# A graph attention layer on one core: x_r and edge attributes in one 64-row product, a last node group of three tiles, all other groups' sums in PSUM, the last group but one from round 772

## The chip, the core and the metric

The kernel runs on one core of one Trainium2 chip. The metric is the device time of one execution in microseconds (us). TensorE (PE) does the matrix products, VectorE (DVE) and ScalarE (ACT) the elementwise work. GpSimd (POOL) issues the indirect DMAs that gather rows by index, and SyncE (SP) issues the other DMAs. PSUM is the memory that PE writes its products to, SBUF the on-chip memory that everything else lies in.

## The reference, cut to what matters

One pre-norm GATv2 layer with a feed-forward part on 12,500 nodes of 128 values and 400,000 edges with 32 attributes each; the edges are sorted by destination. There are 8 heads of 16 channels.

```
h    = relu(layernorm(x)); g = ln1(h)
x_l  = g @ W_l ; x_r = g @ W_r ; e = edge_attr @ W_e
m    = leaky_relu(x_l[src] + x_r[dst] + e, 0.2)      # self loops too, with the mean edge attribute
a    = softmax of (m . att) per head over the edges of a destination
h2   = h + segment_sum(x_l[src] * a) + bias
out  = x + h2 + gelu(ln2(h2) @ W1 + b1) @ W2 + b2
```

## The kernel before, in words

Nodes are padded to 98 tiles of 128. A prologue normalizes all nodes, writes the rows of x_l to DRAM (`xl_dram`) and gathers 116 x 128 raw rows of x. Then `window_edges` works through the edges in 782 pairs. A pair is two units of 256 edges, 512 columns, four gathers of 128 rows. The 29 pairs whose raw rows were gathered in the prologue need no gather: their rows are computed on the way and loaded from `late_dram`.

The order is written out by hand (`tc.manual_schedule`): one Python loop over rounds `r`. In each round every stage works on the pair that `stages` gives it, and each engine takes its instructions in the order in which the loop emits them. For pair c:

- `gather` (round c-4, POOL, L915): four indirect DMAs into `xs`, a ring of 12 buffers. `windows` (round c-3, SP): loads of edge attributes `ea`, of destination differences `dlw` (once for four pairs) and of a window of x_r rows (`xrw`).
- `place` (round c-1, DVE, L945): a one-hot matrix `ne`, bfloat16, of 112 partitions by 512 columns. It compares `dlw` with a column `nid`.
- `combine` (round c, PE): the sum z in PSUM, from four transposes of `xs` (L959), `xrw` x `ne` (L962, bfloat16, x_r held as three bfloat16 parts) and `we_z` x `ea` (L963, float32, two instructions).
- `slope` and `bend` (round c+1): ACT scales z (L969), DVE takes the maximum m (L974).
- `score` (round c+2, PE): `ab` = `farw` x `ne` (L980, which pushes out edges of other units) plus `negrep` x m (L981). `ab` has two PSUM banks in turn.
- `lowest` and `weigh` (round c+3): DVE takes the minimum of `ab` (L988), ACT the exponentials (L999).
- `turn` (c+4, PE, L1007), `keep_turned` (c+5, ACT, L1012), `collect` (c+6, PE, L1021), `own_heads` (c+7, DVE, L1030 and L1036), `put` (c+7, SP, L1047): the weights are turned and multiplied with the rows; each unit's record goes to DRAM (`state`).

Beside this run side jobs, in rounds of their own: `xr_steps` compute x_r for the next four tiles (with a split into three bfloat16 parts, of which `third`, L597, is a DVE subtraction), `raw_steps` do the same for the raw pairs' x_l, and sums over the edge attributes run in the first 196 rounds. When all edges of a group of four node tiles are done, the group's `steps` run over some 20 rounds: `f_load`, scores of the self loops, `f_out` and `f_h` (the softmax sums), statistics, and the feed-forward part up to `f_store` and `f_put`. `f_biases` (L1110, L1112) adds `bias` to `h_sb` and `b2` to `f_x`, and `f_rest` (L1211) adds `h_sb` to `f_x`. There are 25 groups: 24 of four tiles and a last one of two. The last group but one runs a shorter table, `soon`, from round 780 (776 with its loads). The last one runs `last_steps`: loads and self scores in rounds 770 to 775, and the rest, one step after the other, once the last record is in DRAM (round 790).

Of the kernel before, what the change touches and what calls it, by code (L numbers as in the profile page):

```python
# [22 lines left out]
P = 128  # L23
# [17 lines left out]
NS = 3  # L41
# [10 lines left out]
XR_STEPS = 8  # L52
# [49 lines left out]
def node_groups(nt):  # L102

    return [(t, min(GN, nt - t)) for t in range(0, nt, GN)]
# [34 lines left out]
def tile_gnn(  # L139
# [43 lines left out]
    xs_dram = dram.tile([NT * P * NS, P], BF16, name="xs_dram")  # L183
    xs_t = xs_dram.rearrange("(t p s) f -> p t s f", p=P, s=NS)
# [22 lines left out]
    ident_b = const.tile([P, P], BF16, name="ident_b")  # L207
# [12 lines left out]
    we_z = const.tile([P, QP, P], F32, name="we_z")  # L220
    NC3 = NS * CW
# [12 lines left out]
    we_sb = build.tile([P, P], F32, name="we_sb")  # L234
    EP = RU * U
# [10 lines left out]
    def load_consts():  # L246
# [4 lines left out]
        nc.sync.dma_start(we_sb, bass.AP(tensor=w_e.tensor, offset=w_e.offset, ap=[[P, DE], [0, QP], [1, P]]))  # L251
        nc.sync.dma_start(w1_sb, w1)
# [79 lines left out]
    own = build.tile([P, NW, H], F32, name="own")  # L332
    last = build.tile([P, NW, H], F32, name="last")
    third = build.tile([P, CW], F32, name="third")
    in_order = build.tile([P, CW], F32, name="in_order")
    unit = build.tile([P, 1], F32, name="unit")
    fq = build.tile([P, QP, DE], F32, name="fq")
# [3 lines left out]
    def count_up():  # L341
        iota(nc, nh, [[-1, H], [-H, NW]], 0, 1)
        iota(nc, own, [[-1, NW], [0, H]], -NC3, 1)
        iota(nc, last, [[0, NW], [0, H]], -NC3 - NW, 1)
        iota(nc, third, [[-NS, CW]], 0, 1)
        iota(nc, in_order, [[1, CW]])
        iota(nc, unit, [[0, 1]], -NC3, 1)
        iota(nc, fq, [[-1, QP], [-QP, DE]], 0, 1)
        iota(nc, place, [[1, RU]], 0, RU)
        iota(nc, fh, [[-1, H], [-H, C]], 0, 1)  # L350

    def edge_constants():
        nc.vector.tensor_scalar(win_sb, first_sb[:, 0:NU:UP], float(NS * P * 2), None, op0=OP.mult)
        nc.vector.tensor_scalar(first_sb, first_sb, float(H * SH * 4), None, op0=OP.mult)
        nc.vector.tensor_copy(ident_b, ident)
# [14 lines left out]
        nc.vector.tensor_scalar(farw, own, BIG, None, op0=OP.mult)  # L370
        group_range(nc, build, third, NS, CW)
        nc.vector.tensor_mul(third, third, in_order)
        nc.vector.tensor_reduce(nid, third, AX.X, OP.add)
        nc.vector.tensor_scalar(unit, unit, 0.0, None, op0=OP.max)
        nc.vector.tensor_add(nid, nid, unit)
        nc.vector.tensor_scalar(fq, fq, 0.0, None, op0=OP.is_equal)
        qm = build.tile([P, QP], F32, name="qm")
        nc.vector.tensor_reduce(qm, fq, AX.X, OP.max)
        for q in range(QP):
            nc.vector.tensor_scalar(we_z[:, q, :], wer, qm[:, q : q + 1], None, op0=OP.mult)  # L380
# [167 lines left out]
    def xr_steps(pool, bank):  # L548
# [37 lines left out]
        def first(d):  # L586
            n = d["n"]
            xr = d["b"][:, 0 : n * P].rearrange("p (t f) -> p t f", f=P)
            d["parts"] = pool.tile([P, GN, NS, P], BF16, name="xr_parts")[:, 0:n]
            nc.scalar.copy(d["parts"][:, :, 0, :], xr)  # L590
            nc.vector.tensor_sub(tile_of(d, "left", 0), xr, d["parts"][:, :, 0, :])

        def second(d):
            nc.scalar.copy(d["parts"][:, :, 1, :], d["left"][:, 0 : d["n"]])

        def third(d):
            nc.vector.tensor_sub(d["parts"][:, :, 2, :], d["left"][:, 0 : d["n"]], d["parts"][:, :, 1, :])  # L597

        def store(d):
            nc.sync.dma_start(xs_t[:, d["ts"], :, :], d["parts"])  # L600

        return norm, turn, turned, times, first, second, third, store

    def raw_steps(pool, bank):
# [68 lines left out]
        def rows(d):  # L673
            d["xl"] = pool.tile([P, GN, XW], F32, name="l_xl", tag="xr_parts")[:, 0 : d["n"]]
# [90 lines left out]
    with tc.If(fast == 1) as cmp:  # L765
        window_edges(
            tc, n_edges, ea_t, NT, NE, NUE, ident, ident_b, wer, we_z, negrep, diag, nid, farw, bias_r, b2_r, w1_sb, w2_sb,
            cols, xl_dram, xl_t, xs_dram, xs_t, dc_dram, du_dram, late_dram, state, clear, xr_steps, qs, raw_steps, raw, x_t, out_t, h_sb, src_sb, first_sb, win_sb,
        )
    with cmp.Else():  # L770
        any_edges(
            tc, n_edges, dst, dst_tiles, ea_t, NT, NG, NCH, CPP, CP, ident, w_e, att, att_c, bias_r,
            xl_dram, xl_t, xs_t, xr_steps, qs, h_sb, src_sb,
        )
        feed_forward(tc, NT, NG, ident, b2_r, w1_sb, w2_sb, cols, x_t, out_t, h_sb)
# [52 lines left out]
def whole(nc, out, parts):  # L828

    nc.vector.tensor_add(out, parts[:, :, 0, :], parts[:, :, 1, :])  # L830
    for s in range(2, NS):
        nc.vector.tensor_add(out, out, parts[:, :, s, :])


# [9 lines left out]
def window_edges(  # L844
    tc, n_edges, ea_t, NT, NE, NUE, ident, ident_b, wer, we_z, negrep, diag, nid, farw, bias_r, b2_r, w1_sb, w2_sb,
    cols, xl_dram, xl_t, xs_dram, xs_t, dc_dram, du_dram, late_dram, state, clear, xr_steps, qs, raw_steps, raw, x_t, out_t, h_sb, src_sb, first_sb, win_sb,
# [12 lines left out]
    NN = 6  # L859
    NV = WAHEAD + 3  # L860
    NC3 = NS * CW
# [13 lines left out]
    with ExitStack() as es:  # L875
# [13 lines left out]
        xrw = [once.tile([P, P], BF16, name=f"xrw{i}") for i in range(NV)]  # L889
        nes = [once.tile([P, EPR], BF16, name=f"ne{i}") for i in range(NN)]  # L890
        for t in xrw:
            nc.gpsimd.memset(t, 0.0)
        for t in nes:
            nc.vector.memset(t, 1.0)
# [28 lines left out]
        def windows(c):  # L923
            if c % QP == 0:
                ea = load.tile([P, EPR], F32, name="ea")
                nc.sync.dma_start(
                    ea, bass.AP(tensor=ea_t.tensor, offset=ea_t.offset + c * EPR, ap=[[e_pad, DE], [EPR, QP], [1, EPR]])
                )
                n = min(QP * EPR, dc_dram.shape[0] - c * EPR)
                dlw = load.tile([NC3 + NW, QP * EPR], BF16, name="dlw")  # L930
                for rs, dl in ((slice(0, NC3), dc_dram), (slice(NC3, NC3 + NW), du_dram)):
                    nc.sync.dma_start(dlw[rs, :n], dl[c * EPR : c * EPR + n].partition_broadcast(rs.stop - rs.start))
                at = words(win_sb[0:1, c : c + QP], (NT * P - CW) * NS * P * 2)
                for i in range(c, min(c + QP, n_pr)):
                    pairs[i].update(ea=ea, dlw=dlw, win=at[i - c])
            nc.sync.dma_start(
                xrw[c % NV][0:NC3, :].bitcast(U8), rows_at(xs_dram, pairs[c]["win"], NC3, P * 2)
            )

        def place(c):  # L940

            d = pairs[c]
            n, q = sum(edges_of(c)), c % QP * EPR
            ne = nes[c % NN]
            nc.vector.tensor_scalar(  # L945
                ne[0 : NC3 + NW, :n],
                d["dlw"][:, q : q + n],
                nid[0 : NC3 + NW],
                None,
                op0=OP.is_equal,  # L950
            )
            d["ne"] = ne

        def combine(c):
# [7 lines left out]
            nc.tensor.matmul(z[:, :e], xrw[c % NV], d["ne"][:, :e], start=False, stop=False)  # L962
# [860 lines left out]
```

## Time and profile before

| | us |
|---|---|
| three runs | 4013.26, 4021.4, 4024.89; median 4021.4 |
| the profiled execution | 4009.67 |
| its span | 4007.9 |

The page splits the span into busy time by engine, 40 slices, DMA queues, the chain of work that ended last, the costliest groups of instructions and the DMA issues. A row of a group says: line, engine, operation, tiles out and in, count, then busy time, mean of one in ns, and the idle time of the engine ahead of it with what ended it. A row of the timeline says: start, duration, engine, line, operation. The granted clock of TensorE is 0.956 over the span.

| slices of the page | first two | rest |
|---|---|---|
| PE busy, tenths | 3, 4 | 8 or 9, and 7 in the last |
| DVE busy, tenths | 7, 4 | 5 to 7 |
| POOL busy, tenths | 7, 7 | 7, and 3 in the last |

### The profile page before, as it was taken

To read this page: it belongs to the slowest core of one execution; us is meant where nothing else is said; L and a number is where in the kernel's file an instruction comes from. 1 tells how busy PE (TensorE), PEld (TensorE's weight loads), DVE (VectorE), ACT (ScalarE), POOL (GpSimd) and SP (SyncE) were. 2 spreads that over 40 slices of the span, in tenths; PEclk is the share of its full clock that TensorE was granted. 3 is DMA by queue.
4 is the path that set the end of the run, shared out by engine and by line. 5 is a ranking of instruction groups with operands and counts; after the bars stand their busy time and mean duration, and the time that the engine had idled before them with its cause. 6 is when DMAs were issued, how large, how long until landed. Compare 5 with 4: busy or idle time off the path is not lost.

```text
span 4007.9 us, 63213 instructions
## 1 busy us (share of the span) xinstructions
PE 3550.4 (89%) x19116; PEld 2520.3 (63%) x19315; DVE 2540.8 (63%) x5940; ACT 2185.3 (55%) x4768; POOL 2993.8 (75%) x3153
## 2 busy tenths in 40 slices
PE   3488998998889999998998999999989989998997
PEld 3356666666666666666666666666666666666665
DVE  7467676767666665665666666566666656566565
ACT  7445555555555545555555555556555455554554
POOL 7777777777777777777777777777777777777773
PEclk7699999999999999999999999999999999999998
DMA  7677787677656655555556556555556555655553
GB/s 215 207 186 193 197 206 201 173 178 170 166 122 132 128 125 127 126 124 125 118 126 133 125 124 128 128 125 120 127 118 130 125 115 123 127 118 124 125 116 72
DMA packets 650171, 566.02 MB, mean 141 GB/s; under 512 B 385806, under 2 KB 524925, under 8 KB 649581
## 3 DMA queue, kind: packets, MB, share of 16 engines
q1 hardware_dynamic: 549245, 344.42, 34.1%
q0 software_dynamic: 100000, 217.32, 27.4%
q8 instruction: 156, 2.56, 0.3%
q14 instruction: 194, 1.59, 0.1%
q10 hardware_dynamic: 576, 0.13, 0.0%
HBM read 492.44 MB, written 69.02 MB: 140 GB/s over the span
## 4 chain that ended last, share of the span: by engine, by line
PE 43%; DMA 21%; POOL 20%; issue 11%; DVE 1%; ACT 0%; SPq 0%; POOLq 0%; DVEq 0%; ACTq 0%
DMA xs<-xl_dram,src_sb 21%; POOL xs L915 20%; PE z L963 10%; PE acc L1021 9%; PE ab L981 8%; PE pt_ps L1007 5%; PE z L959 5%; PE z L962 2%; PE ab L980 1%; PE acc L1295 1%; PE acc L1270 1%; PE acc L1131 0%; PE pt_ps L581 0%; PE pt_ps L668 0%; PE acc L1126 0%
## 5 line engine op out<-in xcount | busy, mean ns | idle before, releaser
L915 POOL DMA_INDIRECT xs<-xl_dram,src_sb x3009 | 2873.2, 955 | 917.2 <-issue 792.8
L999 ACT ACTIVATE p<-ab,rec 128x256 f32<-128x256 f32 x1563 | 655.2, 471 | 1057.4 <-DVE rec L988 1041.1
L1030 DVE TENSOR_TENSOR own<-acc,diag 128x272 f32<-128x272 f32 x782 | 344.1, 440 | 1077.3 <-PE acc L1021 1061.6
L1021 PE MATMUL acc<-xs,pt 128*128 128x136 f32 x6250 | 881.0, 286 | 2.4 <-DVE f_o L1190 2.2
L959 PE MATMUL z<-ident,xs 128*128 128x128 f32 x3125 | 561.9, 283 | 342.6 <-DMA xs<-xl_dram,src_sb 338.6
L959 PEld LDWEIGHTS z<-ident,xs 128*128 128x128 f32 x3125 | 398.4, 142 | 741.1 <-DMA xs<-xl_dram,src_sb 410.8
L963 PE MATMUL z<-ea,we_z 128*128 128x512 f32 x1564 | 839.7, 620 | 0.1
L981 PE MATMUL ab<-m,negrep 128*128 128x512 f32 x1564 | 802.3, 595 | 11.4 <-issue 1.3
L1021 PEld LDWEIGHTS acc<-xs,pt 128*128 128x128 f32 x6250 | 809.3, 197 | 3.8 <-issue 3.5
L1012 ACT COPY pt<-pt_ps 128x512 f32<-128x512 f32 x782 | 455.1, 582 | 591.0 <-PE pt_ps L1007 581.6
L1007 PEld LDWEIGHTS pt_ps<-ident,p 128*128 128x128 f32 x3125 | 410.9, 147 | 439.3 <-issue 394.4
L988 DVE TENSOR_REDUCE rec<-ab 128x2 f32<-128x512 f32 x781 | 540.4, 692 | 124.0 <-PE ab L981 116.6
L974 DVE TENSOR_TENSOR m<-z,zs 128x512 f32<-128x512 f32 x782 | 532.8, 681 | 87.2 <-ACT zs L969 85.7
L969 ACT ACTIVATE zs<-z 128x512 f32<-128x512 f32 x782 | 472.6, 604 | 44.1 <-DMA xs<-xl_dram,src_sb 35.7
L1007 PE MATMUL pt_ps<-ident,p 128*128 128x128 f32 x3125 | 492.7, 283 | 1.2 <-ACT p L999 1.2
L1036 DVE TENSOR_REDUCE rec<-own 128x34 f32<-128x272 f32 x782 | 340.9, 436 | 26.7
L963 PEld LDWEIGHTS z<-ea,we_z 128*128 128x128 f32 x1564 | 308.1, 197 | 32.7
L981 PEld LDWEIGHTS ab<-m,negrep 128*128 128x128 f32 x1564 | 301.6, 193 | 40.2 <-issue 4.3
L962 PE MATMUL z<-ne,xrw 128*128 128x512 bf16 (+1 forms) x781 | 304.8, 390 | 0.2 <-DMA xs<-xl_dram,src_sb 0.2
L945 DVE TENSOR_SCALAR ne<-dlw,nid 112x512 bf16<-112x512 bf16 x782 | 288.2, 369 | 13.5 <-DMA dlw<-du_dram 13.5
L980 PE MATMUL ab<-ne,farw 128*128 128x512 bf16 x585 | 223.8, 383 | 2.5 <-ACT p L999 1.6
L277 POOL DMA_INDIRECT raw<-in_x,src_raw x116 | 116.6, 1005 | 38.0 <-issue 34.1
(246 smaller groups left out, 2317.4 us busy)
## 6 DMA issues: line engine op xcount, KB each, us to landing
dlw<-dc_dram SPq DMA_DIRECT2D x196, 384.0 KB
ea<-in_ea_t SPq DMA_DIRECT2D x196, 256.0 KB
ea_s<-in_ea_t SPq DMA_DIRECT2D x98, 512.0 KB
xs<-xl_dram,src_sb POOLq DMA_INDIRECT x3009
state<-rec SPq DMA_DIRECT2D x1563, 9.0 KB
xrw<-xs_dram SPq DMA_DIRECT2D x782, 24.0 KB
state<-empty SPq DMA_DIRECT2D x28, 504.0 KB
f_st<-state SPq DMA_DIRECT2D x48, 288.0 KB
```

The lines of the kernel that those rows point to most:

```text
L915: nc.gpsimd.indirect_dma_start(out=xs[:, j, :], out_offset=None, in_=xl_dram, in_offset=bass.IndirectOffsetOnAxis(ap=src_sb[:, c * KP + j ...
L959: nc.tensor.matmul(z[:, j * P : (j + 1) * P], d["xs"][:, j, 0:P], ident, start=(j == 0), stop=False, is_transpose=True)
L962: nc.tensor.matmul(z[:, :e], xrw[c % NV], d["ne"][:, :e], start=False, stop=False)
L963: nc.tensor.matmul(z[:, :e], we_z[:, c % QP, :], d["ea"][:, :e], start=False, stop=True)
L969: nc.scalar.activation(d["zs"][:, :e], d["z"][:, :e], AF.Copy, scale=SLOPE)
L974: nc.vector.tensor_tensor(d["m"][:, :e], d["z"][:, :e], d["zs"][:, :e], op=OP.max)
L981: nc.tensor.matmul(ab[:, :e], negrep.rearrange("p n h -> p (n h)"), d["m"][:, :e], start=False, stop=True)
L988: nc.vector.tensor_reduce(d["rec"][:, :, CX], d["ab"].rearrange("p (u e) -> p u e", e=U), AX.X, OP.min)
L999: nc.scalar.activation(d["p"][:, us], d["ab"][:, us], AF.Exp, bias=d["rec"][:, i, CX:SH], scale=-1.0)
L1007: nc.tensor.transpose(d["pt_ps"][:, js], d["p"][:, js], ident)
L1012: nc.scalar.copy(d["pt"][:, :e], d["pt_ps"][:, :e])
L1021: nc.tensor.matmul(d["acc"][:, i, :], d["pt"][:, j * P : (j + 1) * P], d["xs"][:, j, :], start=(j == js[0]), stop=(j == js[-1]),)
```

## The change

x_r is kept in DRAM as float32 rows (`xr_dram`) in place of three bfloat16 parts, so `xr_steps` has six steps and no subtractions. The window of x_r (32 rows) is loaded into rows 32 to 63, or 96 to 127, of a stationary tile `zw` whose other rows hold W_e. The one-hot of a pair is written in float32 by `place` into the same 64 partitions of `ea`, so that one float32 product over 64 rows takes the place of L962 and L963. The one-hot of the units, for `farw`, is a second DVE operation on 96 partitions in bfloat16, once for two pairs. Its product becomes a stage of its own, `apart`, emitted behind `combine` over the other 64 partitions, and opens the bank `ab` there. Loads for four pairs are two of `ea` and four of `dl`, where one of `ea` and two of `dlw` were; the window of a pair has 16 KB where it had 24. The clearing of the window tiles goes from POOL to DVE copies. `bias`, `h_sb` and `b2` are added in PSUM, in `f_h` and `f_store`, for all groups but the last. The groups are now 3, 23 x 4 and 3 tiles; `soon` starts from round 772 (768 with its loads), and the last group's loads and self scores stand in rounds 772 to 777.

```diff
 def node_groups(nt):
-    return [(t, min(GN, nt - t)) for t in range(0, nt, GN)]
+    last = GN - 1
+    first = (nt - last) % GN
+    at = ([0] if first else []) + list(range(first, nt, GN))
+    return [(t, n - t) for t, n in zip(at, at[1:] + [nt])]
...
-        def first(d):
-            nc.scalar.copy(d["parts"][:, :, 0, :], xr)
-            nc.vector.tensor_sub(tile_of(d, "left", 0), xr, d["parts"][:, :, 0, :])
-        def second(d):
-            nc.scalar.copy(d["parts"][:, :, 1, :], d["left"][:, 0 : d["n"]])
-        def third(d):
-            nc.vector.tensor_sub(d["parts"][:, :, 2, :], d["left"][:, 0 : d["n"]], d["parts"][:, :, 1, :])
+        def keep(d):
+            n = d["n"]
+            d["xr"] = pool.tile([P, GN, XW], F32, name="xr_rows")[:, 0:n, 0:P]
+            nc.scalar.copy(d["xr"], d["b"][:, 0 : n * P].rearrange("p (t f) -> p t f", f=P))
...
-        for t in xrw:
-            nc.gpsimd.memset(t, 0.0)
+        for t in zws:
+            nc.vector.tensor_copy(t, weh)
...
         def place(c):
-            nc.vector.tensor_scalar(
-                ne[0 : NC3 + NW, :n],
-                d["dlw"][:, q : q + n],
-                nid[0 : NC3 + NW],
-                None,
-                op0=OP.is_equal,
-            )
+            rs = slice(d["half"].start + DE, d["half"].stop)
+            nc.vector.tensor_scalar(d["ea"][rs], d["dl"][rs], nid[rs], None, op0=OP.is_equal)
+            if c % 2 == 0:
+                nc.vector.tensor_scalar(d["ne"][0 : P - DE], d["dl"][0 : P - DE], nid[0 : P - DE], None, op0=OP.is_equal)
...
-            nc.tensor.matmul(z[:, :e], xrw[c % NV], d["ne"][:, :e], start=False, stop=False)
-            nc.tensor.matmul(z[:, :e], we_z[:, c % QP, :], d["ea"][:, :e], start=False, stop=True)
+            rs = d["half"]
+            nc.tensor.matmul(z[:, :e], d["zw"][rs], d["ea"][rs, :e], start=False, stop=True)
...
+        def apart(c):
+            d, e = pairs[c], sum(edges_of(c))
+            d["ab"] = ps2.tile([P, EPR], F32, name="ab")
+            rs = d["other"]
+            nc.tensor.matmul(
+                d["ab"][:, :e], farw.rearrange("p n h -> p (n h)")[rs], d["ne"][rs, :e], start=True, stop=False
+            )
...
         def score(c):
-            nc.tensor.matmul(ab[:, :e], farw.rearrange("p n h -> p (n h)"), d["ne"][:, :e], start=True, stop=False)
-            nc.tensor.matmul(ab[:, :e], negrep.rearrange("p n h -> p (n h)"), d["m"][:, :e], start=False, stop=True)
+            nc.tensor.matmul(d["ab"][:, :e], negrep.rearrange("p n h -> p (n h)"), d["m"][:, :e], start=False, stop=True)
...
         def f_h(d):
             nc.vector.tensor_add(d["sum"], d["sum"], d["o2"])
+            if d is not end:
+                up = d["sum"].rearrange("p (t f) -> p t f", f=P)
+                nc.vector.tensor_add(up, up, bias_r[:, None, :].to_broadcast([P, d["n"], P]))
             nc.vector.tensor_add(hb, hb, d["sum"])
...
         def f_store(d):
-            nc.vector.tensor_add(y, up, d["x"][:, 0:n])
+            if d is end:
+                nc.vector.tensor_add(y, up, d["x"][:, 0:n])
+                return
+            nc.vector.tensor_add(up, up, d["x"][:, 0:n])
+            nc.vector.tensor_add(up, up, h_sb[:, d["ts"], :])
+            nc.vector.tensor_add(y, up, b2_r[:, None, :].to_broadcast([P, n, P]))
...
             (0, combine),
+            (2, apart),
             (4, turn),
...
             (-4, f_load),
-            (-2, f_biases),
-            (8, f_rest),
             (-3, f_order),
...
         last_steps = (
-            (-20, f_load),
+            (-18, f_load),
```

179 lines of the change are left out of this document (86 added, 93 removed).

## The prediction

> **What bounds the kernel now.** The chain of waits ends in a mixture (PE 43%, DMA 21%, POOL 20%), so I looked for the engine that never waits for another. On the page that is POOL:
>
> ```profile
> span 4007.9 us, 63213 instructions
> L915 POOL DMA_INDIRECT xs<-xl_dram,src_sb x3009 | 2873.2, 955 | 917.2 <-issue 792.8
> L959 PE MATMUL z<-ident,xs 128*128 128x128 f32 x3125 | 561.9, 283 | 342.6 <-DMA xs<-xl_dram,src_sb 338.6
> ```
>
> PE waits 338.6 us in all for gathered rows; POOL's idle time is 917.2/3009 = 0.305 us a gather, the same from first to last in its timeline:
>
> ```profile
> 160.50 0.93 POOL L892 MEMSET xrw<- 128x128 bf16 x6 [2.11 <-issue]
> 161.59 0.95 POOL L915 DMA_INDIRECT xs<-xl_dram,src_sb  x1 [0.15 <-issue]
> 3949.60 0.94 POOL L915 DMA_INDIRECT xs<-xl_dram,src_sb  x1 [0.30 <-issue]
> 3950.84 0.95 POOL L915 DMA_INDIRECT xs<-xl_dram,src_sb  x1 [0.30 <-PE acc L1131]
> ```
>
> From 161.59 to 3951.79 POOL does nothing but gather. That is 3790.2 us, 4.85 a pair over 782 pairs. What PE saves inside this stretch is hidden. Time can come from three places only: the gathers' own length, the start, and what follows the last gather (56 us).
>
> A normal gather takes 0.944 us (0.94 or 0.95 in the rows) and with its pause of 0.305 begins every 1.249. 3009 of them would be busy 2840.5 us; the row has 2873.2, so **32.7 us are extra**. The timeline shows when:
>
> ```profile
> 2127.29 0.69 DVE L1110 TENSOR_TENSOR h_sb<-h_sb,bias_r 128x512 f32<-128x512 f32 x1
> 2127.90 0.69 DVE L1112 TENSOR_TENSOR f_x<-f_x,b_r 128x512 f32<-128x512 f32 x1
> 2128.03 1.37 POOL L915 DMA_INDIRECT xs<-xl_dram,src_sb  x1 [0.30 <-DMA xs<-xl_dram,src_sb]
> ...
> 3788.77 2.22 POOL L915 DMA_INDIRECT xs<-xl_dram,src_sb  x1 [0.30 <-issue]
> 3788.88 0.69 DVE L1110 TENSOR_TENSOR h_sb<-h_sb,bias_r 128x512 f32<-128x512 f32 x1
> 3789.49 0.69 DVE L1112 TENSOR_TENSOR f_x<-f_x,b_r 128x512 f32<-128x512 f32 x1
> ...
> 2169.57 0.69 DVE L1207 TENSOR_TENSOR h_sb<-h_sb,ab 128x512 f32<-128x512 f32 x1
> 2169.67 0.94 POOL L915 DMA_INDIRECT xs<-xl_dram,src_sb  x1 [0.30 <-issue]
> ...
> 225.22 0.34 DVE L945 TENSOR_SCALAR ne<-dlw,nid 112x512 bf16<-112x512 bf16 x1
> 225.32 1.06 POOL L915 DMA_INDIRECT xs<-xl_dram,src_sb  x1 [0.30 <-issue]
> ```
>
> In the first case the DVE sum ends at 2128.59, and the gather is 0.43 too long: it stood still from 0.13 us after its start until the sum was done. In the second it stood through two sums in a row. L1207, whose second operand lies in PSUM, is running at the same point and costs the gather nothing. So a DVE sum of two SBUF operands holds up a gather that reaches a point 0.13 us after its start; one with a PSUM operand does not. `place` (L945) holds it too, by at most 0.12 us.
>
> The Trainium skill, page "SBUF — State Buffer", section "Who interferes with whom", has this as a lock on a port that DVE and GpSimd share: two SBUF inputs contend with GpSimd's reads, and copies and tensor_scalar in two-port modes contend throughout. The trace agrees for the first. For the second it shows less than the full block: of 782 runs of L945, each 0.34 us in a period of 1.25, only 61 lengthened a gather.
>
> **Part by part.** *Sums in PSUM, no third part of x_r.* The operations with two SBUF operands that go are, from the groups by shape:
>
> ```profile
> L1110 DVE TENSOR_TENSOR h_sb<-h_sb,bias_r 128x512 f32<-128x512 f32 x24 | 16.4, 682 | 0.0
> L1112 DVE TENSOR_TENSOR f_x<-f_x,b_r 128x512 f32<-128x512 f32 x24 | 16.4, 683 | 0.0
> L1211 DVE TENSOR_TENSOR f_x<-f_x,h_sb 128x512 f32<-128x512 f32 x24 | 16.4, 683 | 0.0
> L597 DVE TENSOR_TENSOR xr_parts<-xr,xr_parts 128x512 bf16<-128x512 f32 x24 | 16.4, 685 | 0.0
> ...
> 270.44 1.43 POOL L915 DMA_INDIRECT xs<-xl_dram,src_sb  x1 [0.30 <-issue]
> 3837.67 1.56 POOL L915 DMA_INDIRECT xs<-xl_dram,src_sb  x1 [0.30 <-issue]
> ```
>
> 47 gathers, from the one at 270.44 to the one at 3837.67, have one of these four over their point; together they are 28.8 us too long. Beside L945 alone stand the 61, 3.7 us together; 0.2 is left over. As a check: L1110 and L1112 together last 1.29 us, a whole period, so one gather always meets them and waits half of it, 24 x 0.6 = 15; L1211 and L597 meet one with 0.68/1.25 and cost 0.34 then, 48 x 0.19 = 9. So 24 is the mean, 32.7 the most; I take **-28.8**. The three sums that replace them have one PSUM and one SBUF operand, as L1207, and cost DVE the same 0.69.
>
> *Place.* One DVE operation a pair becomes one of 32 x 512 from bfloat16 to float32 (A), and for even pairs behind it one of 96 x 512 in bfloat16 (B, as L945). No row shows A; two rows of single-operand operations bound its form:
>
> ```profile
> 66.93 0.21 DVE L132 TENSOR_SCALAR fh<-fh 128x128 f32<-128x128 f32 x1
> 40.27 2.15 DVE L398 CAST df<-dc 112x3841 f32<-112x3841 int32 x1
> ```
>
> (2.15-0.21)/3713 columns is 0.52 ns, so A takes about 0.41 us (0.34 at L945's pace, 0.68 at that of a sum). Since L945 adds at most 0.12, it must start 0.21 to 0.09 before the gather to block it: a window of 0.12, 75 expected hits, 61 counted. For A the window is 0.41-0.13-0.09 = 0.19: 119 hits of 0.095, times 61/75, 9 us. B, half as often as L945, 1.8. Against 3.7 now: **+7**. Lower bound: A doesn't hold the port at all, -1.9. Upper bound: B follows without a gap and the gather waits for it too: in even rounds 59 hits by A, each 0.30 longer, 14 more: +21. I take +7: each of the 61 waited for one operation of this kind, none for two.
>
> *POOL's start.* The six memsets leave: from 160.50 to 161.59, **-1.0** (0 if the first gather then waits for the same buffers).
>
> *PE.* L962 goes, and `apart` runs early. PE's free round is in the timeline:
>
> ```profile
> 3937.21 0.60 PE L959 MATMUL z<-ident,xs 128*128 128x128 f32 x4
> 3937.65 0.38 PE L962 MATMUL z<-ne,xrw 128*128 128x512 bf16 x1
> 3937.86 1.02 PE L963 MATMUL z<-ea,we_z 128*128 128x512 f32 x2
> 3938.72 0.60 PE L1007 MATMUL pt_ps<-ident,p 128*128 128x128 f32 x4
> 3940.30 1.02 PE L981 MATMUL ab<-m,negrep 128*128 128x512 f32 x2
> 3941.16 0.60 PE L959 MATMUL z<-ident,xs 128*128 128x128 f32 x4
> 3941.36 0.69 DVE L988 TENSOR_REDUCE rec<-ab 128x2 f32<-128x512 f32 x1 [0.17 <-DMA xrw<-xs_dram]
> 3942.09 0.84 ACT L999 ACTIVATE p<-ab,rec 128x256 f32<-128x256 f32 x2 [1.65 <-DVE rec L988]
> ```
>
> 3.95 us a round; without L962 3.74. But `apart` needs the bank that `weigh` (L999) reads last, and everything behind it on PE (turn, collect, score) queues. From the end of L981 (3941.32) to that of L999 (3942.93) is 1.61; from L1007 to the end of L981, with `farw`'s product, 2.60. The loop is 4.26 with 0.05 for a semaphore. That is longer than before, and below POOL's 5.0 of a gathered pair: **0**. The 64-row products are bounded by 0 and the present 0.86 for L963; the slack covers either.
>
> The Trainium skill, page "TensorEngine Tiling (Array Packing)", section "Tiling Modes", speaks against it: a change of tiling mode drains TensorE. With two changes a round and 0.16 us of tail each (1.02 less 0.86) the loop would be 4.6, still under 5.0. No run so far shows a 64-row product.
>
> The extra DMA issues fall to SP, three in four rounds; they start three rounds ahead.
>
> *What follows the last gather.*
>
> ```profile
> 3963.84 1.02 PE L981 MATMUL ab<-m,negrep 128*128 128x512 f32 x2
> 3981.83 0.30 DVE L1036 TENSOR_REDUCE rec<-own 128x17 f32<-128x136 f32 x1
> 3986.34 0.39 SPq L1310 DMA_DIRECT2D out<-f_yo  x1
> 3986.78 1.04 SPq L1097 DMA_DIRECT2D end_st<-state  x2
> ...
> L1200 DVE TENSOR_TENSOR ab<-ab,f_o 128x512 f32<-128x512 f32 x24 | 16.8, 699 | 0.8
> L1200 DVE TENSOR_TENSOR ab<-ab,end_o 128x256 f32<-128x256 f32 x1 | 0.4, 433 | 0.0
> ```
>
> From the score of pair 780 (done 3964.86) to the last record (3982.13) 17.3 us pass; the pair's own steps (L988, L999, L1007, L1012, L1021, L1030, L1036) need about 5.7, the rest is the last group but one on DVE and ACT. Its output also stands on SP ahead of `end_st`, about 2.4. From round 772 all of this lies before the last gather: -14 at most. There it delays PE instead: some 9 us of DVE work in the rounds around pair 776, which has no gather and so gives POOL 5 us of lead. I give 9 back: **-5** (-14 to +4). The last group has three tiles: its six sums grow by half of 699-433, 0.8; a tile more of statistics (0.43), of scaling (0.44), of products (1.0), and shares of the rest, 1.0: **+3.7** (3 to 4.5).
>
> Sum: -28.8 + 7 - 1 - 5 + 3.7 = **-24.1**. The profiled execution took 4009.7, so 3985.6; the runs' median lies 11.7 above it, so 3997.
>
> **The rivals.** (1) *A does not hold the port:* 7 + 1.9 less, 3988. For it: only one SBUF input, 32 partitions. Against: L945 has one too and does hold it. (2) *B is chained to A,* as L1112 to L1110: 14 more, 4011. (3) *The drain gives nothing back and the four sums were hit above their mean in this execution* (24, not 28.8; +4, not -5): 14 more, 4011. (4) *Slower:* PE now waits for gathers and DVE follows PE, so `place` can lock to the gathers' period. If A and B stand before half of the 391 even rounds' gathers, at 0.095 + 0.30 each, they cost 77 against the 7 taken: 4067. It decides from about 43 us, a quarter of the even rounds, on. Against it: L945 hit 61 of 782, no more than chance gives. (5) *Slower, PE:* if drains and waits bring the loop to 5.2, the 0.35 above 4.85 times 782 pairs is 270 us: about 4270; it needs 0.9 more than the rows give.
>
> **How the numbers follow.** Forecast 0.58, (1) 0.10, (2) 0.13, (3) 0.06, (4) 0.08, (5) 0.05. A run of this kernel tells 0.3% (12 us) from no change. The forecast and (1) are faster but for a twentieth: 0.63. (2), (3) and that rest are the same: 0.24. (4) and (5): 0.13. With all adverse bounds save (4) and (5) the sum is +5 (4027), with all good ones -47 (3975); the ends together hold little, so the range is 3977 to 4025.
>
> **What would show it.** L915's mean falls from 955 to about 948 ns, and no gather over 1.5 us stands in the groups' rounds. Lengthened gathers stand beside the new `place` alone: under 0.4 each means no chain. The last gather ends near 3929. POOL's idle stays 0.305 a gather; if it grows, PE or the row buffers bind, and the forecast is wrong. PE's wait for `xs` stays above zero. `end_st` is issued with no `out` just ahead of it.

## The result, and the profile after

The changed kernel takes 4007.3 us, the median of 7 runs (4006.8 to 4009.6), against 4021.4 before: ratio 0.9968, 95% interval 0.9958 to 0.9978. The interval excludes no change; the 0.3% that the prediction took as the least that can be told from no change lies inside it. The time is 10 us above the forecast, and it came by another route. The page of the profiled execution after, which took 4008.3 us itself:

```profile
span 4006.6 us, 63160 instructions
L903 POOL DMA_INDIRECT xs<-xl_dram,src_sb x3009 | 2872.3, 955 | 918.0 <-issue 774.6
L953 PE MATMUL z<-ident,xs 128*128 128x128 f32 x3125 | 593.5, 286 | 317.5 <-DMA xs<-xl_dram,src_sb 281.6
L944 DVE TENSOR_SCALAR ea<-dl,nid 32x512 f32<-32x512 bf16 x782 | 392.5, 502 | 30.3 <-DMA dl<-dc_dram 5.0
L946 DVE TENSOR_SCALAR ne<-dl,nid 96x512 bf16<-96x512 bf16 x391 | 146.5, 375 | 14.3 <-DMA dl<-du_dram 1.8
```

The gathers (L903, before L915) still set the time: POOL's pause is 918.0/3009 = 0.305 us, as before, so neither PE nor a buffer holds POOL back. But their mean length stays at 955 ns, where 948 was forecast, and the last one ends at 3949.16, where 3929 was. `place` now stands in two rows, A (L944) at 502 ns and B (L946) at 375.

The timeline after shows which gathers are too long now. Columns are start, length, engine and line:

```profile
3935.00 0.48 DVE L944 TENSOR_SCALAR ea<-dl,nid 32x512 f32<-32x512 bf16 x1
3935.10 1.19 POOL L903 DMA_INDIRECT xs<-xl_dram,src_sb  x1 [0.30 <-DMA xs<-xl_dram,src_sb]
3935.51 0.35 DVE L946 TENSOR_SCALAR ne<-dl,nid 96x512 bf16<-96x512 bf16 x1
...
3106.43 1.04 POOL L903 DMA_INDIRECT xs<-xl_dram,src_sb  x1 [0.31 <-issue]
3106.86 0.49 DVE L944 TENSOR_SCALAR ea<-dl,nid 32x512 f32<-32x512 bf16 x1
```

In the first case A runs over the point 0.13 us after the gather's start. A ends at 3935.48, and 3935.48 - 3935.10 - 0.13 = 0.25 is what the gather has too much: it is held until A ends. B starts 0.03 us later and costs it nothing more. In the second case A starts 0.43 us after the gather and ends 0.92 after it, and the gather is 0.10 too long. That is a second point; reckoned from A's end in the same way it lies 0.82 us after the gather's start. Over the whole trace 164 gathers were held by A at the first point, 20.0 us together and none by over 0.26, and 64 more at the second, 5.0 us (over the trace's own undisturbed gather, 946.0 ns). All but a few of these fit A's end less the point to within 0.025 us. Beside B alone stands nothing that counts. Before it was 28.8 beside the sums, 3.6 beside L945 and some 1 us beside shorter operations.

At the second point the gather can also hold A:

```profile
3927.54 0.94 POOL L903 DMA_INDIRECT xs<-xl_dram,src_sb  x1 [0.30 <-issue]
3928.00 0.73 DVE L944 TENSOR_SCALAR ea<-dl,nid 32x512 f32<-32x512 bf16 x1
```

A starts 0.46 us after the gather, takes 0.73 us in place of 0.48, and the gather loses nothing. 122 runs of A that start between 0.45 and 0.69 us into a gather end 1.19 us after its start, wherever they began. This is most of why the mean of A is 502 ns. So A holds a gather at the second point only if it starts before 0.45 and ends after 0.82. L945, with 0.34 us, is too short for that. The sums of two SBUF operands are long enough, but in the profile before seven of them (L597, L1110, L1211) that started 0.37 to 0.45 us into a gather cost it nothing.

One gather stands beside a sum of two SBUF operands, with 0.4 us, and six beside L1180, whose operands lie in SBUF too and whose result goes to PSUM, with 0.4 us together. The one is among the last group's own sums, which stay outside PSUM:

```profile
3940.28 0.55 DVE L1109 TENSOR_TENSOR h_sb<-h_sb,bias_r 128x384 f32<-128x384 f32 x1
3940.35 1.31 POOL L903 DMA_INDIRECT xs<-xl_dram,src_sb  x1 [0.30 <-DMA xs<-xl_dram,src_sb]
3940.75 0.55 DVE L1111 TENSOR_TENSOR end_x<-end_x,b_r 128x384 f32<-128x384 f32 x1
```

L1111 begins 0.08 us before L1109 ends, as L1112 begins 0.08 before L1110 ends, and yet this gather is held by L1109 alone.

The rows around the start and the end of the gathers after:

```profile
157.96 0.94 POOL L281 DMA_INDIRECT raw<-in_x,src_raw  x1 [0.30 <-issue]
159.20 0.95 POOL L903 DMA_INDIRECT xs<-xl_dram,src_sb  x1 [0.31 <-issue]
...
3948.22 0.94 POOL L903 DMA_INDIRECT xs<-xl_dram,src_sb  x1 [0.30 <-PE ab L981]
3968.18 0.39 SPq L1315 DMA_DIRECT2D out<-f_yo  x1
3978.09 0.30 DVE L1035 TENSOR_REDUCE rec<-own 128x17 f32<-128x136 f32 x1
3981.72 0.93 SPq L1096 DMA_DIRECT2D f_st<-state  x2
4001.78 0.39 SPq L1315 DMA_DIRECT2D out<-f_yo  x1
```

With the rows of before, the two profiles compare like this:

| stretch | before, us | after, us | difference |
|---|---|---|---|
| to the first gather of the loop | 161.59 | 159.20 | -2.4 |
| extra length of gathers over the trace's own undisturbed one | 33.3 | 25.7 | -7.6 |
| 3009 undisturbed gathers (943.8 and 946.0 ns) | 2839.9 | 2846.6 | +6.7 |
| pauses between gathers | 917.0 | 917.7 | +0.7 |
| last gather's end to the issue of the last group's state | 34.98 | 32.56 | -2.4 |
| from there to the end | 21.14 | 24.86 | +3.7 |
| span | 4007.91 | 4006.58 | -1.3 |

The two profiles differ by 1.3 us, the medians by 14. So two things had to be found out: whether the extra lengths are what they look like, and why before's profile lies 12 us under its median.

### The profile page after: what moved, and what is told of

Its sections match the earlier page's. It is cut to its first block, busy times and chain, and to the rows that moved or that the text cites. A ratio compares the mean times of both kernels' runs of the same rounds, so it can differ in the third digit from the quotient of the medians.

```text
span 4006.6 us, 63160 instructions
## 1 busy us (share of the span) xinstructions
PE 3558.9 (89%) x18434; PEld 2243.9 (56%) x18435; DVE 2817.3 (70%) x6281; ACT 2182.0 (54%) x4746; POOL 2991.2 (75%) x3146
## 4 chain that ended last, share of the span: by engine, by line
PE 38%; POOL 21%; DMA 20%; issue 14%; DVE 4%; SPq 1%; ACT 1%; POOLq 0%; DVEq 0%; ACTq 0%
POOL xs L903 19%; DMA xs<-xl_dram,src_sb 17%; PE z L957 9%; PE acc L1020 9%; PE ab L981 7%; PE pt_ps L1006 6%; PE z L953 4%; POOL raw L281 2%; DMA state<-rec 1%; PE acc L1295 1%; DVE rec L987 1%; DMA raw<-in_x,src_raw 1%; SPq L923 1%; DVE m L976 1%; DMA zw<-xr_dram 1%
## 5 line engine op out<-in xcount | busy, mean ns | idle before, releaser
L903 POOL DMA_INDIRECT xs<-xl_dram,src_sb x3009 | 2872.3, 955 | 918.0 <-issue 774.6
L957 PE MATMUL z<-ea,zw 64*128 64x512 f32 x1564 | 901.3, 657 | 2.5 <-DMA zw<-xr_dram 2.5
L953 PE MATMUL z<-ident,xs 128*128 128x128 f32 x3125 | 593.5, 286 | 317.5 <-DMA xs<-xl_dram,src_sb 281.6
L953 PEld LDWEIGHTS z<-ident,xs 128*128 128x128 f32 x3125 | 407.7, 143 | 760.9 <-DMA xs<-xl_dram,src_sb 427.2
L981 PE MATMUL ab<-m,negrep 128*128 128x512 f32 x1564 | 829.2, 613 | 0.0
L1006 PEld LDWEIGHTS pt_ps<-ident,p 128*128 128x128 f32 x3125 | 338.5, 144 | 614.3 <-issue 508.1
L1006 PE MATMUL pt_ps<-ident,p 128*128 128x128 f32 x3125 | 531.9, 294 | 0.9 <-ACT pt L1011 0.8
L944 DVE TENSOR_SCALAR ea<-dl,nid 32x512 f32<-32x512 bf16 x782 | 392.5, 502 | 30.3 <-DMA dl<-dc_dram 5.0
L964 PE MATMUL ab<-ne,farw 64*128 64x512 bf16 x782 | 306.7, 392 | 21.6 <-ACT p L998 20.7
L957 PEld LDWEIGHTS z<-ea,zw 64*128 64x128 f32 x1564 | 234.6, 188 | 118.4 <-issue 59.2
L981 PEld LDWEIGHTS ab<-m,negrep 128*128 128x128 f32 x1564 | 251.3, 199 | 3.0 <-issue 3.0
L946 DVE TENSOR_SCALAR ne<-dl,nid 96x512 bf16<-96x512 bf16 x391 | 146.5, 375 | 14.3 <-DMA dl<-du_dram 1.8
L281 POOL DMA_INDIRECT raw<-in_x,src_raw x116 | 115.7, 997 | 39.3 <-issue 34.2
```

Of the source, the lines that this page charges most:

```text
L903: nc.gpsimd.indirect_dma_start(out=xs[:, j, :], out_offset=None, in_=xl_dram, in_offset=bass.IndirectOffsetOnAxis(ap=src_sb[:, c * KP + j ...
L944: nc.vector.tensor_scalar(d["ea"][rs], d["dl"][rs], nid[rs], None, op0=OP.is_equal)
L953: nc.tensor.matmul(z[:, j * P : (j + 1) * P], d["xs"][:, j, 0:P], ident, start=(j == 0), stop=False, is_transpose=True)
L957: nc.tensor.matmul(z[:, :e], d["zw"][rs], d["ea"][rs, :e], start=False, stop=True)
L981: nc.tensor.matmul(d["ab"][:, :e], negrep.rearrange("p n h -> p (n h)"), d["m"][:, :e], start=False, stop=True)
L1006: nc.tensor.transpose(d["pt_ps"][:, js], d["p"][:, js], ident)
```

## The experiments

The theory: gathers set the time; the sums in PSUM gave back what stood beside them; A, which makes gathers wait, took most of it again. The rivals: `place` costs nothing and the gain went elsewhere; a gather waits for a chain of operations and not for one; before's first profile was a lucky execution.

The twelve runs fell on four chips: e1 to e6 on chip 1, e7 on chip 2, e8 to e11 on chip 3, e12 on chip 4 (numbered in the order of the runs). For the first profile, the profile after and the runs beside these two no chip is on record. On chips 1 and 4 every kernel, the one before too, took some 4800 us; before took 4020 on chip 2 and 4013 on chip 3.

**The kernel before, again (no edit).**

> The kernel before, unchanged, for a second profile. In its first profile the undisturbed gather took 944 ns, and so did the gathers of raw rows ahead of the loop; in the profile after both take 947, though nothing that the change touches stands beside the raw gathers. Theory (the 3 ns belong to the chip or the execution, not to the change): in this profile the undisturbed gather may take 947 too, the span is then 4007.9 + 3009 x 0.0025 = 4015 to 4022, and the extra over the normal gather stays at 24 to 36 us. Rival (the first profile was lucky with the sums of two SBUF operands): the undisturbed gather stays at 944 and the extra over it is 40 us or more.

Measured: 4795.2, ratio 0.9994 (0.9985 to 1.0003). This is another regime, and the expectation didn't foresee it. From the page, and from the table of waits (what waited for what, us in total, times, longest):

```profile
L915 POOL DMA_INDIRECT xs<-xl_dram,src_sb x3009 | 2881.2, 958 | 1633.6 <-issue 791.6
```

```profile
POOL xs L915 <- issue: 791.6, 2591, 0.8
POOL xs L915 <- remote: 325.3, 150, 3.2
POOL xs L915 <- PE acc L1021: 216.8, 87, 14.9
```

POOL stands idle 716 us more than in the first profile, in 389 pauses of mostly 2 us at the start of a pair; the profile names PE as what ends most of them. But in the loop there are also 388 stretches of over 0.31 us in which PE, DVE, ACT and POOL all stand still at once, 273 us together, and the first profile has none. So it isn't PE alone that is late. Gathers don't bind on this chip, and what stops all engines there was not found. The gathers' own lengths can still be read: 944.1 ns undisturbed and 40.4 us of extra length, 38.4 of it beside the sums. Those are the numbers of the rival (944, and 40 or more); e10 below decides it on a chip where gathers bind.

**The three sums in PSUM alone, in the kernel before.** In `f_h` and `f_store` as in the change; L597 stays.

```diff
-            (-2, f_biases),
-            (8, f_rest),
...
+            if d is not end:
+                up = d["sum"].rearrange("p (t f) -> p t f", f=P)
+                nc.vector.tensor_add(up, up, bias_r[:, None, :].to_broadcast([P, d["n"], P]))
             nc.vector.tensor_add(hb, hb, d["sum"])
```

> The kernel before with one part of the change: the three sums per node group with two SBUF operands become sums into PSUM; the third part of x_r, place, the products and the groups stay. Theory (the sums cost what the gathers beside them were too long): in the first profile the gathers beside these three lines were about 25 us too long together, L597 keeps some 4; so -25 us against before (ratio 0.9938), between -18 and -30. Rival (the sums were hit above their mean in that one execution): 24 x 0.6 + 24 x 0.19 = 19, so -19 (0.9953). Rival (the sums cost nothing, the gathers only shift): within 4 us of before.

> The kernel of e2_sums_alone again, since there the gathers lost 34 us of extra length (40.7 to 6.5) while the time stayed, on a chip on which every engine stood still every 12 us and POOL had 717 us more of idle time. Where gathers follow each other at 1.25 us, the theory has the time fall by what the gathers lose: -19 to -30 us against before (0.9926 to 0.9953). Rival (PE follows at its own pace and the gathers only run ahead): within 4 us of before, with POOL's idle time larger by what the gathers lost.

> The kernel of e2_sums_alone (before with the three sums in PSUM, L597 kept) on such a chip. Theory: -25 us of gathers beside the sums (-19 at their mean), so 3995 to 4001 against before at 4020, ratio 0.9938 to 0.9953; this is then below the changed kernel, which gives the gain back through place. Rival (gathers are not what sets the time): 0.999 to 1.001.

Measured: 0.9997 (0.9988 to 1.0006) and 0.9996 (0.9987 to 1.0005) on chip 1, 3989.7 or 0.9941 (0.9928 to 0.9955) on chip 3. The first run's page says why nothing came of it there:

```profile
L915 POOL DMA_INDIRECT xs<-xl_dram,src_sb x3009 | 2847.0, 946 | 1666.0 <-issue 786.4
```

The gathers lost 34.2 us (2881.2 to 2847.0) and POOL's idle time took 32.4 of them (1633.6 to 1666.0). The same gain on a chip where gathers bind is time: 23.4 us by the medians. The page of e10 below has the gathers of before on chip 3 at 2874.3 us busy; with the sums alone they are

```profile
L915 POOL DMA_INDIRECT xs<-xl_dram,src_sb x3009 | 2850.2, 947 | 917.2 <-issue 782.1
```

24.1 us less, at the same idle time. What is left beside L597 is 4.4 us. So the sums were worth what the prediction gave them, and gathers do set the time there: what they lose in length, the kernel loses in time. The ratio of this kernel lies under that of the whole change (0.9968, and 0.9972 in e7).

**A of place in another form: columns in steps of 256.**

```diff
-            nc.vector.tensor_scalar(d["ea"][rs], d["dl"][rs], nid[rs], None, op0=OP.is_equal)
+            ea, dl = (d[k][rs].rearrange("p (h e) -> p e h", h=2) for k in ("ea", "dl"))
+            nc.vector.tensor_scalar(ea, dl, nid[rs], None, op0=OP.is_equal)
```

> The changed kernel with the 32-row operation of place (A) walking its 512 columns in steps of 256 instead of in a row; same work and same output. Theory (A holds up the gathers that reach their point under it, 25.5 us in the profile after): if A in this form leaves the port alone, the gathers beside it are 0.95 us again and the time falls by about 25 us (3982), though A itself grows to 0.6 us or more; if it holds the port for its whole 0.6 us, the window grows from 0.26 to 0.38 us and the time rises by 782 x 0.38/1.249 x 0.19 - 25 = +20 (4027). Rival (place costs the gathers no more than L945 did, and the gain went elsewhere): within 4 us of the changed kernel either way.

Measured: 1.0032 (1.0019 to 1.0045), on a chip where the time doesn't decide. The groups by shape:

```profile
L903 POOL DMA_INDIRECT xs<-xl_dram,src_sb x3009 | 2889.9, 960 | 1656.6 <-issue 784.3 <-remote 269.5 <-PE acc L1021 229.7
L945 DVE TENSOR_SCALAR ea<-dl,nid 32x512 f32<-32x512 bf16 x782 | 562.8, 720 | 29.7 <-issue 4.5
```

A takes 720 ns and still holds the gathers, up to 0.37 us each and 49.2 us in all. That an A in this form leaves the gathers alone is refuted. The single hold is longer than with A of 0.48 us (0.37 against 0.26 at most), as the theory has it, but it falls short of the 0.50 that 0.72 less 0.22 would give. Whether more gathers are held can't be said, since the changed kernel itself was not run on chip 1.

**A twice.** The line with `op0=OP.is_equal` into `ea` stands there two times.

> The changed kernel with operation A of place issued twice in a row (the second writes the same values). Theory (each A holds up a gather by itself, with a gap of 0.04 us between two in which a waiting gather gets through): twice the cost, +20 to +26 us against the changed kernel (4027 to 4033). Rival (a chain: the gather waits for both, as it did for L1110 and L1112): window 0.96 - 0.22 = 0.74 us, 782 x 0.74/1.249 x 0.37 = 171 us in place of 25, +146 (4153). Rival (place costs nothing worth naming): within 4 us.

Measured: 1.0041 (1.0029 to 1.0053), on the same chip. Extra length 11.1 us, 92 gathers, none over 0.26. The chain's 146 us is refuted. The second A did not cost another 20 either; but how often one A meets a gather between such pauses isn't known on this chip, so of this expectation only the chain is answered.

**A in two halves.**

```diff
-            nc.vector.tensor_scalar(d["ea"][rs], d["dl"][rs], nid[rs], None, op0=OP.is_equal)
+            for i in range(2):
+                es = slice(i * EPR // 2, (i + 1) * EPR // 2)
+                nc.vector.tensor_scalar(d["ea"][rs, es], d["dl"][rs, es], nid[rs], None, op0=OP.is_equal)
```

> The changed kernel with operation A of place cut into two of 256 columns each; same values. In the profile after, A lasts 0.48 us where nothing stretches it, and a gather is held only if A starts 0.09 to 0.35 us before it. Theory (a gather waits for the one operation that runs over its point, and an operation shorter than some 0.22 us could never be in its way): a half lasts about 0.21 + 0.27/3 = 0.30, its window is 0.08 and its mean hold 0.04, so 1564 x 0.08/1.249 x 0.04 = 4 us in place of 20.4: about -16 us against the changed kernel (3991 where that takes 4007), gathers held up by at most 0.10. Rival (chain: the gather waits for both halves): no less than now, 4007 or a little more. Rival (place costs the gathers nothing worth naming): 4007. On a chip where gathers don't set the time, as in the first four runs here, the time says nothing and the gathers' extra length over the normal one has to decide: 2 to 6 us by the theory.

> The kernel of e5_place_halves (A of place in two halves) on a chip where gathers follow each other at 1.25 us. There the changed kernel took 4008.2 (0.9972 of before). Theory (a gather is held only by the one operation over its point): the extra length beside place falls from some 25 us to 7 or less (7.1 in all in e5_place_halves), so the time falls by 16 to 20 us: 3988 to 3992, ratio 0.992 to 0.993. Rival (a chain over the halves, or place costs nothing worth naming): 4004 to 4012.

Measured: on chip 1 1.0036 (1.0023 to 1.0048) with 7.0 us of extra length; on chip 3 3993.0, ratio 0.9953 (0.9939 to 0.9967), with 17.6 us. From the page of the second run, and from its timeline:

```profile
L903 POOL DMA_INDIRECT xs<-xl_dram,src_sb x3009 | 2857.6, 950 | 917.4 <-issue 775.0
L946 DVE TENSOR_SCALAR ea<-dl,nid 32x256 f32<-32x256 bf16 x1564 | 513.9, 366 | 28.3 <-DMA dl<-dc_dram 3.0
```

```profile
1797.52 0.62 DVE L946 TENSOR_SCALAR ea<-dl,nid 32x256 f32<-32x256 bf16 x2
1797.88 1.08 POOL L903 DMA_INDIRECT xs<-xl_dram,src_sb  x1 [0.30 <-issue]
```

The second half ends at 1798.14, 0.26 after the gather began, and the gather is 0.14 too long. That is the most that any gather lost beside `place`. The direction is the theory's, the size half of it: beside A stand 12.9 us against 24.2 in e11 on the same chip, but B, which held next to none in the profile after, now holds 73 gathers for 4.6. A half takes 0.344 us where nothing stretches it, not 0.30, so its window, the stretch of start times from which it catches a gather, is 0.12 us and not 0.08. No half holds a gather at the second point; they are too short for it, like L945.

**The changed kernel and the kernel before, again.**

> The changed kernel, unchanged. On the chip of the first six runs here no kernel was bound by its gathers, so nothing there says how the changed kernel stands to before; this run gives the baseline for the extra length of gathers beside place (L944). Theory (A meets gathers at random): where gathers follow each other at 1.25 us, 782 x 0.26/1.249 = 163 gathers are held, 0.13 us each, 21 us, as in the profile after (164, 20.4), and the time is some 0.3% under before. On the chip of the first six runs, where gathers wait for buffers at the start of a pair, the phases are not random: then between 9 us (as with A twice) and 33 us (as with A in steps), and the time is 0.3 to 0.4% above before, since the three variants of it were (1.0032, 1.0041, 1.0036), set by PE. Rival (the variants' own edits made them slower there): at or under 1.000.

> The kernel before on such a chip, for a profile that stands nearer to its median of some 4020 than the first one (4009.7). Theory (the first one had gathers of 944 ns, the profiles after 947, ahead of the loop too): undisturbed gathers of 946 to 947 ns, which is 6 to 9 us, and 24 to 40 us of extra length beside the sums; tail and start as before (56 and 161.6 us). Rival (the difference lies elsewhere, in the start or the tail): gathers of 944 ns and a first or last gather that is 5 us or more off.

Measured: the changed kernel 4008.2 against 4019.8, ratio 0.9972 (0.9961 to 0.9984), on chip 2; 25.0 us of extra length beside A. The kernel before, on chip 3, 4010.9 in one run, beside a median of 4013.1:

```profile
L915 POOL DMA_INDIRECT xs<-xl_dram,src_sb x3009 | 2874.3, 955 | 917.1 <-issue 783.9
```

Its undisturbed gather takes 943.8 ns, with 34.4 us of extra length: the first profile over again. The theory is wrong on the gather, and right on the extra. In e7 it is 945.7, in the profile after 946.0. The gathers of raw rows ahead of the loop, the same code in both kernels, have medians of 944 ns in the one set and 947 in the other. So the rival of e10 is right that its gathers stay at 944, but not for the reason it gave: nothing is off in start or tail. The variants of the changed kernel on chip 3 (e8, e11) have gathers of 944 too, so the 2 to 3 ns go with the chip, not with the change. Before takes 4013 on chip 3 and 4020 on chip 2, and 3009 times 2 to 3 ns is 6 to 9. That the first profile came from a chip like the one and the three runs beside it from one like the other fits this, but isn't shown.

**The node groups of before, in the changed kernel.**

```diff
-    last = GN - 1
-    first = (nt - last) % GN
-    at = ([0] if first else []) + list(range(first, nt, GN))
-    return [(t, n - t) for t, n in zip(at, at[1:] + [nt])]
+    return [(t, min(GN, nt - t)) for t in range(0, nt, GN)]
```

> The changed kernel with the node groups of before: 24 of four tiles and a last one of two, the last but one from round 780. In the profile after, 32.6 us lie between the last gather's end and the issue of the last group's state, and 24.9 from there to the end; before it was 35.0 and 21.1. Theory (the groups alone set both): 35.0 and 21.1 again, +2.4 - 3.7 = -1.3 us: the new groups are no gain. Rival (the first part is set by PE's slower loop and not by the groups, so that moving the group did help): 37 us or more ahead of the issue, and a time 1 us or more above the changed kernel's.

Measured: 4001.2, ratio 0.9972 (0.9962 to 0.9981), on chip 3. Its timeline has the last gather end at 3940.44, then

```profile
3976.04 0.70 DVE L1307 TENSOR_TENSOR acc<-acc,f_x 128x512 f32<-128x512 f32 x1 [3.91 <-PE acc L1292]
3976.78 0.70 DVE L1308 TENSOR_TENSOR acc<-acc,h_sb 128x512 f32<-128x512 f32 x1
3977.51 0.69 DVE L1309 TENSOR_TENSOR f_yo<-acc,b_r 128x512 f32<-128x512 f32 x1
3978.23 0.39 SPq L1312 DMA_DIRECT2D out<-f_yo  x1
3978.67 1.06 SPq L1093 DMA_DIRECT2D f_st<-state  x2
```

38.2 us to the state's issue and 22.4 to the end, where e8, with the new groups and A in halves, has 31.8 and 25.1 on the same chip. So the new groups save about 60.6 - 56.9 = 3.7 us (2.8 to 3.2 against the 57.4 and 57.9 of the profile after and of e7). The rival is right in this stretch. Its other sign, a longer time, can't be read: the changed kernel was not run on chip 3, and the ratio here is that of e7. The profiles of e11 and e8 differ by 10.4 us, of which 6.5 is the length of the gathers and 3.7 the groups, so here too time off the gathers is time off the kernel.

**The parts that paid, together:** the kernel of the sums alone, with the new groups and last steps and with `xrw` cleared on DVE.

```diff
         for t in xrw:
-            nc.gpsimd.memset(t, 0.0)
+            nc.vector.memset(t, 0.0)
```

> Of the change only the parts that paid by themselves: the kernel of the sums alone (three parts of x_r, place in one operation, loop as before), with the new node groups and the clearing of the row buffers on VectorE instead of POOL. Theory (terms add: sums alone 0.9941 of before; the six memsets kept POOL 2.9 us between the last raw gather and the first of the loop; the new groups took 38.2 + 22.4 of the old groups to some 32.6 + 24.9, -3.1): another -6 us under the sums alone, so 0.9926 of before (3983 where before takes 4013, 3990 where it takes 4020), first gather of the loop 2 to 3 us earlier, extra length of gathers as with the sums alone (6 to 10 us). Rival (start and tail only shift a wait, since the first pairs wait for their rows and the last group for its state anyway): 0.9938 to 0.9945. On a chip where every kernel takes 4800: within 0.2% of before, by either.

Measured: 1.0034 (1.0022 to 1.0047) on chip 4, with 6.3 us of extra length. So it stays open what these parts add up to where gathers bind. On chips 1 and 4 all four kernels with the new groups are 0.3 to 0.4% slower than before, and the sums alone on chip 1 are not. This kernel differs from the sums alone by the groups, the last group's rounds and tiles, and the clearing, so the loss seems to come with these; but the sums alone were not run on chip 4, and by what way was not found.

## Why the prediction was right, and where it was not

*What bounds the kernel.* This was right. POOL's pause is 0.305 us before and after, and in e9 24.1 us off the gathers were 23.4 off the time.

*Sums in PSUM, -28.8.* This was right in place and size. Beside these lines 29.6 us of extra length stood in e10, 4.4 in e9, where L597 alone is left, and 0.4 after.

*Place, +7.* This is the step that failed, and by size: 25.0 us beside A and B in place of L945's 3.6 is **+21.4**. The mechanism was the one named: A holds a gather if it starts 0.09 us or more before it and ends after the point 0.13 us into it, so its window is its length less 0.22. Three things were wrong. A takes 0.48 us undisturbed, not 0.41, so the window is 0.26 us and not 0.19, and the mean hold about 0.13 and not 0.095. The hits were scaled down by the 61 of 75 that L945 happened to have; by the bare window 782 x 0.26/1.249 = 163 are due, and 164 came. And the second point cost 5.0 that no row of before showed. The prediction's upper bound, +21, is what was measured, but by luck: its reason, B chained to A, is wrong, since the held gather goes ahead in the 0.03 us between A and B (3935.10 above). What makes a chain stays open. In the three profiles of before all 47 gathers that L1110 caught waited for L1112 too, and L1112 had begun 0.08 us before L1110 ended; but so had L1111 at 3940.75 above, and there, as in e7, the gather did not wait for the second.

*POOL's start, -1.0.* The profiles have -2.4. The row of the six memsets had 2.11 us of idle time ahead of it, and that left with them. The last raw gather of before stands in its timeline as

```profile
157.45 0.94 POOL L277 DMA_INDIRECT raw<-in_x,src_raw  x1 [0.30 <-issue]
```

From there to the first of the loop at 161.59 were 4.14 us; after it is 1.24, so 2.9 went. The last raw gather itself starts 0.5 later after the change. On chip 3 too it starts later with the new kernel (157.76 and 158.11 in e8 and e11, 157.19 and 156.98 in e10 and e9), so this goes with the change; which part of it does so was not tested.

*PE, 0.* This was right in its effect. A round after the last gather, up to the start of the next, in the profile after:

```profile
3955.25 0.60 PE L953 MATMUL z<-ident,xs 128*128 128x128 f32 x4
3955.78 0.69 PE L957 MATMUL z<-ea,zw 64*128 64x512 f32 x1
3955.79 0.39 PE L964 MATMUL ab<-ne,farw 64*128 64x512 bf16 x1
3956.31 0.59 PE L957 MATMUL z<-ea,zw 64*128 64x512 f32 x1
3956.83 0.66 PE L1006 MATMUL pt_ps<-ident,p 128*128 128x128 f32 x4
...
3959.97 0.60 PE L953 MATMUL z<-ident,xs 128*128 128x128 f32 x4
```

From L953 to L1006 pass 1.58 us; before, from L959 to L1007, it was 1.51, without the product of `farw`, which is in it now. This round also holds L1270 and takes 4.72, under POOL's 5.0. A round without L1270 takes 3.86 (the rounds of L953 at 3934.07 and 3937.93), where the row before had 3.95. So the loop of 4.26 that the prediction reckoned, with `apart` waiting for its bank, doesn't show, and neither does the 4.6 that it drew from the Trainium skill, page "TensorEngine Tiling (Array Packing)", section "Tiling Modes"; how much of the 1.58 is a drain, no run shows. The same section says that different tiles can run at once. There the trace agrees as to the start: the product of `apart` on 64 rows starts 0.01 us after that of `combine` on the other 64. Whether that saves time stays open: from the first of the two to L1006 pass 1.05 us, and L962 and L963 took 1.07 together before.

*What follows the last gather, -5.* Up to the issue of the last group's state the profiles have -2.4. Moving the last group but one gave more than predicted (38.2 to 31.8 us in e11 and e8), but the sums in PSUM had first made that stretch longer, from 35.2 (e10) to 38.0 (e9): three sums of 0.74 us now stand behind that group's products, where one stood. The prediction costed them as equal work on DVE and did not look whose output waits behind them.

*The last group, +3.7.* This was right: 21.14 to 24.86 us.

*From the profile to the median, +11.7.* This was no constant to be added. Before's first profile has gathers of 943.8 ns, as chip 3 has, where before takes 4013; the shown median is 4021, near that of chip 2, where gathers take 945.7. With its terms as measured, -7.6 for the extra length of gathers, -2.4, -2.4 and +3.7, the change is worth some 9 us once the gathers' undisturbed length is taken out, and 12 to 14 by the medians. Before's runs spread over 8 us on one chip and its profile lies 2 under its median there; the rest of the gap stays open. Some 9 us are 0.22%, less than the 0.3% that the prediction asked for: that the time fell by 14 as forecast in sign, and lies well inside the range, is in part luck.

*The rivals.* The time (4007) is nearer to that of rivals (2) and (3), 4011, than to the forecast. (2) fell by its mechanism; (3) too, since the stretch after the last gather gave 2.4 and the sums were hit for 28.8 and 29.6 in two profiles, above the mean of 24. Nothing locked to the gathers' period (4): 164 hits are what chance gives. PE stayed under POOL (5), and A did hold the gathers (1).

## What to carry to other kernels

Where one engine sets the time and an operation on another can hold it up, cost that operation by its window (here its length less 0.22 us) for how often it hits, and by half the window for the mean hold. The cost then grows with the square of the window: a window of 0.12 us (L945) cost 3.6, one of 0.26 (A) cost 20.0 at the same point, 5.6 times as much where the square gives 4.7. The two halves of A cost more than this, 12.9 where it gives 9. So a long operation that replaces a short one can eat a gain that is otherwise real. Take the length from a row of the same types, and where there is none, carry the square through the range. Before a term is added to a median, see whether the profile and the runs come from the same chip: the length of operations that the change didn't touch shows it.

## What the runs showed that was not expected

Two 64-row products on PE started 0.01 us apart (3955.78 and 3955.79 above). A gather can be held at two points, 0.13 and 0.82 us into it. The page "SBUF — State Buffer" of the Trainium skill, section "Who interferes with whom", has the one that issues first keep the shared ports for its whole instruction, where the DVE operation runs in a two-port mode; whether A does, no run shows. The trace agrees that the first one makes the other wait, and for A in its usual form that the gather waits until it ends. For the gather it shows less than the whole instruction: of the 782 runs of A 229 began up to 0.3 us after a gather did, and there A took its usual 0.48 us and the gather lost 1 ns at the mean. A itself waited only in the 122 runs that began 0.45 to 0.69 us into a gather and in 22 that began shortly before one. The undisturbed gather took 943.8 ns on one chip and 945.7 on another, and on two chips all kernels took 4800 us, with POOL's idle time at 1634 to 1716 us in place of 917.
